# Issuing the six loads of each graph from GpSimd's queue instead of SyncE's, in a four-layer graph network

## The chip, the cores and the metric

The kernel runs on one core of a Trainium2 chip. The metric is the device time of one execution in microseconds (us); each kernel was run several times, and a run counts as fast when it lies within 1.5% of the fastest of its kernel. Profiles are of one execution each; its span can differ from the median time by some tenths of a per cent. PE is TensorE (matmuls), PEld its weight load, DVE is VectorE, ACT ScalarE, POOL GpSimd, SP SyncE; the letter q behind a name means that engine's queue of issued DMAs. A DMA lands when its completion is signalled.

## The reference

There are 64 independent graphs with 256 nodes and 512 features. Each goes through four layers, and each layer is added to its input:

```python
def reference(x, adj, nodemask, ...):          # x (64,256,512), adj (64,256,256), float32
    h = maximum(layernorm(x), 0);  x = x + gnn0(h, adj)   # softmax over nodes of sum(q k^T * adj), times v
    h = maximum(layernorm(x), 0);  x = x + gnn1(h, adj)   # 8-head attention, masked by adj
    h = maximum(layernorm(x), 0);  x = x + gnn2(h, adj)   # 8 heads, tanh(adj * xc xp^T), no softmax
    h = maximum(layernorm(x), 0);  x = x + gnn3(h, adj, nodemask)
    return x                                   # ... the weights are left out
```

## The kernel before

Each step of a graph is a small function that emits instructions. A plan gives every step a time, sorts the steps of all graphs by it, and pins each engine to the resulting order, so an engine never overtakes itself. Graphs follow one another by 60.2 of the plan's units, and a graph lives for nearly five periods, so five graphs are in flight.

Steps, with the line numbers by which the profile names them:

```python
@step("load")                                          # xt, adj and blocks are buffers of a pool
def _():
    nc.sync.dma_start(g.take("xt"), x[b]...)           # L633  512 KB
    nc.sync.dma_start(g.take("adj", 4), adj[b]...)     # L634  256 KB
    blocks = g.take("blocks")                          # adj again, in 32x32 blocks
    for q in range(4):
        nc.sync.dma_start(blocks[q*S:(q+1)*S], ...)    # L638  4 x 64 KB, rows of 256 B
@step("at")
    nc.vector.transpose(g.take("at", NC)..., g["blocks"]...)           # L643 VectorE
@step("st0")
    nc.vector.bn_stats(stats[:, c, :], g["xt"][:, c, :])               # L662 VectorE
@step("mxv")                                           # four small operations on mx, 128x16
    nc.vector.tensor_tensor(mx, mx, st["ec"]..., OP.add)               # L861
    nc.vector.tensor_scalar(low, mx, ...)                              # L863
    nc.vector.scalar_tensor_tensor(low, mx, 0.2, low, ...)             # L864
    nc.vector.tensor_tensor(mx, mx, low, OP.max)                       # L865
@step("eg2")
    nc.gpsimd.tensor_tensor(e, e, g["negt"]..., OP.add)                # L897 GpSimd, 2.35 us
@step("tv3")
    nc.vector.tensor_tensor(th[:, s], ..., g["at"], OP.mult)           # L1041 VectorE
@step("yg")
    nc.gpsimd.tensor_tensor(xt, xt, y, OP.add)                         # L1076, one half on GpSimd, one on VectorE
@step("am")                                            # waits for L1041, the last reader of at
    nc.gpsimd.tensor_scalar(g["at"]..., mask_c..., op0=OP.mult)        # L1087 GpSimd
```

In the plan "load" of one graph is at 180.6 of the graph three before it, right behind that graph's "am" at 180.09.

Of the kernel before, what the change touches and what calls it, by code (L numbers as in the profile page):

```python
# [20 lines left out]
NC = N // P  # L21
# [7 lines left out]
S = 32  # L29
# [354 lines left out]
class Graph:  # L384
# [5 lines left out]
    def step(self, name):  # L390
        def add(run):
            self.steps[name] = run
            return run
        return add
# [19 lines left out]
def tile_four_gnn_layers(ctx: ExitStack, tc: tile.TileContext, x, adj, nodemask,  # L414
# [6 lines left out]
    nc = tc.nc  # L421
# [203 lines left out]
    def graph(b):  # L625

        g = Graph(plan)
# [2 lines left out]

        @step("load")
        def _():
            nc.sync.dma_start(g.take("xt"), x[b].rearrange("(p c) d -> p c d", c=NC))  # L633
            nc.sync.dma_start(g.take("adj", 4), adj[b].rearrange("(p c) m -> p c m", c=NC))  # L634

            blocks = g.take("blocks")
            for q in range(4):
                nc.sync.dma_start(blocks[q * S:(q + 1) * S],  # L638
                                  adj[b].rearrange("(a i) (q e) -> q i a e", i=S, q=4)[q])

        @step("at")
# [520 lines left out]
```

## Time and profile before

| | kernel before |
|---|---|
| time, median of the 4 runs beside the kernel after | 3898.6 us (3894.8 to 3902.7) |
| span of the profiled run | 3884.0 us |
| TensorE busy | 98% |
| VectorE busy | 78% |
| GpSimd busy | 33% |
| steady period of a graph | 58.65 us |

The period is the mean of 41 intervals between starts of L643 in the steady part. The prediction below shows the busy shares, the chain of waits and the timelines of one steady graph. Two more lines are needed for later. The first is the table by stretches: window, its length, then busy time with the number of instructions for PE, PEld, DVE, ACT and POOL, then the granted TensorE clock, the DMA share and GB/s.

```profile
1000.00:3400.00 2400.00, 2399.22 (x10973) 1545.78 (x10972) 1912.00 (x4955) 1066.52 (x2050) 805.89 (x697) 1.00 0.63 189
```

TensorE is busy in 2399.22 of 2400 us. VectorE is busy 1912.00 of 2400, which is 46.7 us of a period of 58.65; it waits the other 11.9. The second thing is where VectorE's four small operations stand against GpSimd's work, in the timelines of VectorE and GpSimd (start, duration, us; in brackets the idle time before and what ended it):

```profile
1864.10 0.17 DVE L861 TENSOR_TENSOR mx<-mx,ec 128x16 f32<-128x16 f32 x1
1864.31 0.17 DVE L863 TENSOR_SCALAR mx<-mx 128x16 f32<-128x16 f32 x1
...
1866.72 1.72 POOL L1076 TENSOR_TENSOR xt<-xt,hn 128x512 f32<-128x512 f32 x1 [13.33 <-DMA hn<-sq_d]
```

They take 0.17 us each and are done 1.8 us before GpSimd's next instruction begins.

### The profile page before, as it was taken

Reading aid. Unit: us, or ns where it says so; the run is one execution under the profiler, and the core shown is the slowest. Engines: PE = TensorE matmul, PEld = TensorE weight load, DVE = VectorE, ACT = ScalarE, POOL = GpSimd, SP = SyncE. Lnnn points to the kernel's source line nnn. Section 1 sums busy time; section 2 is a strip of 40 time slices with the busy share of each in tenths; the row PEclk is TensorE's granted clock in tenths of the full one; section 3 lists DMA queues with packets and bytes.
Section 4 is the critical chain, followed back from the end, with each engine's and each line's share of the span. In section 5 each row is a group of like instructions: output and inputs, shape, how many; then the busy total and the mean of one; then the engine's idle time right before and its main releaser. Section 6 shows DMA issues by size and latency. Waiting matters only on the chain.

```text
span 3884.0 us, 53839 instructions
## 1 busy us (share of the span) xinstructions
PE 3809.3 (98%) x17218; PEld 2443.6 (63%) x17218; DVE 3025.1 (78%) x7769; ACT 1668.5 (43%) x3205; POOL 1264.8 (33%) x1100
## 2 busy tenths in 40 slices
PE   7999999999999999999999999999999999999989
PEld 4756666666666666666666666666666666665564
DVE  6887888878877877877888778778777778776774
ACT  2443444444444444444444444444444444443342
POOL 1332333333333323323323323323323333333231
PEclk9999999999999999999999999999999999999989
DMA  7565666665665665666666666666666666665543
GB/s 211 177 190 170 188 189 185 192 194 176 199 196 174 200 195 177 197 194 180 193 190 188 191 190 188 188 189 189 187 188 191 186 190 191 185 190 163 173 149 107
DMA packets 921353, 717.64 MB, mean 185 GB/s; under 512 B 783792, under 2 KB 821232, under 8 KB 896496
## 3 DMA queue, kind: packets, MB, share of 16 engines
q1 hardware_dynamic: 921072, 714.21, 60.8%
q8 instruction: 138, 2.26, 0.2%
q14 instruction: 143, 1.17, 0.1%
HBM read 477.56 MB, written 236.45 MB: 184 GB/s over the span
## 4 chain that ended last, share of the span: by engine, by line
PE 88%; DVE 6%; DMA 3%; issue 1%; SPq 1%; ACT 0%; POOL 0%; DVEq 0%; POOLq 0%; ACTq 0%
PE bank L611 55%; PE bank L921 12%; PE bank L1009 6%; PE bank L1023 5%; PE bank L1095 5%; PE bank L987 3%; DVE junk L851 2%; PE bank L773 1%; DMA sq_d<-sq 1%; DVE sq L617 1%; PE bank L723 1%; DMA all<-m_d 1%; DMA all<-er_d 1%; DVE pair L903 1%; DMA ht<-sq_d 1%
## 5 line engine op out<-in xcount | busy, mean ns | idle before, releaser
L611 PE MATMUL bank<-w_s,ht 128*128 128x256 f32 (+2 forms) x3072 | 949.9, 462 | 14.8 <-DMA ht<-sq_d 9.5
L611 PE MATMUL bank<-wv_s,ht 128*128 128x512 f32 x2048 | 916.6, 595 | 0.0
L611 PEld LDWEIGHTS bank<-w_s,ht 128*128 128x128 f32 x3072 | 595.3, 197 | 352.3 <-issue 237.9
L611 PEld LDWEIGHTS bank<-wv_s,ht 128*128 128x128 f32 x2048 | 393.0, 197 | 415.4 <-issue 400.9
L897 POOL TENSOR_TENSOR pair<-pair,negt 128x1024 f32<-128x1024 f32 x256 | 601.8, 2371 | 51.5 <-ACT pair L890 47.3
L685 ACT ACTIVATE hn<-xt,shift,rstd 128x512 f32<-128x512 f32 x512 | 388.8, 806 | 433.1 <-DVE shift L678 424.4
L921 PEld LDWEIGHTS bank<-feats,pair 128*128 128x128 f32 x4096 | 512.2, 200 | 54.3 <-issue 29.6
L1048 ACT ACTIVATE pair<-pair 128x512 f32<-128x512 f32 x512 | 299.2, 625 | 558.4 <-DVE pair L1041 558.1
L921 PE MATMUL bank<-feats,pair 128*128 128x65 f32 x4096 | 507.5, 283 | 17.5 <-ACT pair L909 17.5
L890 ACT ACTIVATE pair<-all,ec 128x256 f32<-128x256 f32 x1024 | 417.1, 494 | 229.6 <-DMA all<-er_d 225.6
L851 DVE CUSTOM_DVE_ANT_0 junk<-all,adj 128x256 f32<-128x256 f32 x1024 | 446.3, 436 | 38.2 <-DMA all<-er_d 4.8
L611 PE MATMUL bank<-m_s,ht 128*128 128x512 f32 x1024 | 466.3, 599 | 1.9 <-DMA ht<-sq_d 1.2
L673 POOL TENSOR_TENSOR rstd<-rstd,power 128x2 f32<-128x2 f32 x256 | 180.2, 704 | 845.7 <-DVE rstd L669 715.7
L1041 DVE TENSOR_TENSOR pair<-bank,at 128x512 f32<-128x512 f32 x512 | 325.8, 679 | 109.6 <-PE bank L1009 108.7
L617 DVE STREAM_TRANSPOSE sq<-hn 128x512 f32<-128x512 f32 x512 | 338.5, 694 | 59.9 <-ACT hn L685 59.7
L1076 POOL TENSOR_TENSOR xt<-xt,hn 128x512 f32<-128x512 f32 x64 | 108.2, 1691 | 840.8 <-DMA hn<-sq_d 712.1
L903 DVE TENSOR_TENSOR pair<-pair,all 128x1024 f32<-128x1024 f32 x256 | 309.8, 1230 | 57.6 <-DMA all<-m_d 53.7
L662 DVE BATCH_NORM_STATS2 stats<-xt 128x6 f32<-128x512 f32 x512 | 327.2, 681 | 34.2 <-POOL xt L1076 27.5
L611 PEld LDWEIGHTS bank<-m_s,ht 128*128 128x128 f32 x1024 | 195.9, 196 | 208.4 <-issue 202.3
L946 POOL TENSOR_TENSOR xt<-xt,o 128x256 f32<-128x256 f32 x256 | 183.8, 728 | 409.1 <-DVE o L938 300.8
L909 ACT ACTIVATE pair<-pair 128x1024 f32<-128x1024 f32 x256 | 262.3, 1047 | 55.3 <-DVE pair L903 49.9
L1009 PE MATMUL bank<-xc,xpt 64*128 64x256 f32 x2048 | 256.7, 390 | 0.9 <-ACT xc L995 0.7
(74 smaller groups left out, 3793.2 us busy)
## 6 DMA issues: line engine op xcount, KB each, us to landing
sq_d<-sq SPq DMA_DIRECT2D x384, 512.0 KB
ht<-sq_d SPq DMA_DIRECT2D x1024, 128.0 KB
all<-er_d SPq DMA_DIRECT2D x128, 1024.0 KB
all<-m_d SPq DMA_DIRECT2D x64, 1024.0 KB
xt<-in_x_dram SPq DMA_DIRECT2D x64, 512.0 KB
xpt<-sq_d SPq DMA_DIRECT2D x256, 128.0 KB
hn<-sq_d SPq DMA_DIRECT2D x256, 128.0 KB
out_dram<-xt SPq DMA_DIRECT2D x64, 512.0 KB
```

The lines of the kernel that those rows point to most:

```text
L611: nc.tensor.matmul(p, chunk(ht[:, k], c), w[:, k], start=(k == 0), stop=(k == KC - 1))
L617: nc.vector.transpose(sq.rearrange("p (r k i c) -> p c k r i", r=4, k=KC, c=NC)[:, c], t[:, c])
L662: nc.vector.bn_stats(stats[:, c, :], g["xt"][:, c, :])
L685: nc.scalar.activation(hn[:, c, :], g["xt"][:, c, :], AF.Relu, bias=st["shift"][:, c:c + 1], scale=st["rstd"][:, c:c + 1])
L851: nc.vector.tensor_tensor_reduce(junk, g["en"][:, h, :], g["adj"][:, c, :], 1.0, -BIG, OP.add, OP.max, g["mx"][:, c, h:h + 1])
L890: nc.scalar.activation(e[:, s, j, :], g["es"][:, h, :], AF.Prelu, bias=st["ec"][:, j, H + h:H + h + 1], alpha=0.2)
L897: nc.gpsimd.tensor_tensor(e, e, g["negt"][:, None].to_broadcast([P, 2, NC, N]), OP.add)
L903: nc.vector.tensor_tensor(e, e, g["m"][:, 2 * p:2 * p + 2, None, :].to_broadcast([P, 2, NC, N]), OP.subtract)
L921: nc.tensor.matmul(po[:, h % 4, :], chunk(e[:, s, j], i), feats[:, j, h, :], start=(j == 0), stop=(j == NC - 1))
L1009: nc.tensor.matmul(ps[s][:, m, :], chunk(g["xpt"][half, p], m), g["xc"][half, p, :], start=True, stop=True)
L1041: nc.vector.tensor_tensor(th[:, s], g[f"ps{p}{s}"].rearrange("p (m n) -> p m n", m=NC), g["at"], OP.mult)
L1048: nc.scalar.activation(g[f"th{p}"][:, s], g[f"th{p}"][:, s], AF.Tanh)
```

## The change

The intent is to relieve SyncE's queue, which issues all DMAs of the kernel, by giving the loads to an engine that is busy a third of the time.

```diff
         @step("load")
         def _():
-            nc.sync.dma_start(g.take("xt"), x[b].rearrange("(p c) d -> p c d", c=NC))
-            nc.sync.dma_start(g.take("adj", 4), adj[b].rearrange("(p c) m -> p c m", c=NC))
+            nc.gpsimd.dma_start(g.take("xt"), x[b].rearrange("(p c) d -> p c d", c=NC))
+            nc.gpsimd.dma_start(g.take("adj", 4), adj[b].rearrange("(p c) m -> p c m", c=NC))
 
             blocks = g.take("blocks")
             for q in range(4):
-                nc.sync.dma_start(blocks[q * S:(q + 1) * S],
+                nc.gpsimd.dma_start(blocks[q * S:(q + 1) * S],
                                   adj[b].rearrange("(a i) (q e) -> q i a e", i=S, q=4)[q])
```

## The prediction

> **What bounds the kernel now.** I read the page of the profile first, then the timeline of each engine over two neighbouring graphs in the middle, then the waits by tile. The page says that TensorE is the bound and that nothing else is near:
>
> ```profile
> PE 3809.3 (98%) x17218; PEld 2443.6 (63%) x17218; DVE 3025.1 (78%) x7769; ACT 1668.5 (43%) x3205; POOL 1264.8 (33%) x1100
> ...
> PE 88%; DVE 6%; DMA 3%; issue 1%; SPq 1%; ACT 0%; POOL 0%; DVEq 0%; POOLq 0%; ACTq 0%
> ```
>
> The first line is busy time, the second the chain that ended last. TensorE has 2% to gain, so no relief of a queue can be worth more than about 75 us of 3884, and DMA is 3% of the chain. What can move the time is a wait that reaches TensorE in every graph. There are 64 graphs, five in flight, and each engine's instructions run in the fixed order of a plan. In the steady part everything repeats every 58.60 us (the transpose of the adjacency starts at 1849.65 and again at 1908.25).
>
> In the timeline of SyncE's queue, the six loads of one graph are issued here (start, duration, both us):
>
> ```profile
> 1837.32 0.56 SPq L633 DMA_DIRECT2D xt<-in_x_dram  x1
> 1838.22 0.92 SPq L634 DMA_DIRECT2D adj<-in_adj_dram  x1
> 1839.20 1.90 SPq L638 DMA_DIRECT2D blocks<-in_adj_dram  x4
> ```
>
> The first to use them is VectorE, which transposes `blocks` at L643 and takes the statistics of x at L662. From its timeline:
>
> ```profile
> 1847.27 1.25 DVE L1041 TENSOR_TENSOR pair<-bank,at 128x512 f32<-128x512 f32 x2
> 1848.44 1.29 DVE L617 STREAM_TRANSPOSE sq<-hn 128x512 f32<-128x512 f32 x2
> 1849.65 0.67 DVE L643 STREAM_TRANSPOSE at<-blocks 128x512 f32<-128x512 f32 x1
> 1850.24 0.72 DVE L1116 SCALAR_TENSOR_TENSOR bank<-bank,mask_c,cols 128x512 f32<-128x512 f32 x1
> ```
>
> L643 has no idle time before it. The load was issued 1849.65 - 1837.32 = 12.3 us earlier, and by 1841.10 all six were out. Over the whole run L643 waited 0.5 us for its blocks, once. That lead is what the kernel lives on. GpSimd's timeline in the same place:
>
> ```profile
> 1840.20 0.70 POOL L673 TENSOR_TENSOR rstd<-rstd,power 128x2 f32<-128x2 f32 x1 [3.39 <-DVE rstd L669]
> 1848.62 1.83 POOL L1087 TENSOR_SCALAR at<-at,mask_c 128x256 f32<-128x256 f32 x2 [7.72 <-DVE pair L1041]
> 1850.43 0.62 POOL L649 TENSOR_SCALAR adj<-adj 128x512 f32<-128x512 f32 x1
> ```
>
> It sits idle for 7.72 us at L1087, because its queue is in order and that instruction needs VectorE's L1041, which ended at 1848.52.
>
> **What the Trainium skill says.** "DMA: Bandwidth & Descriptors", section "Issuing engines are not separate DMA queues": DMAs of all issuing engines run on the same 16 DMA engines and interleave, so another issuer saves only issue time. Here that is 0.56 + 0.92 + 1.90 = 3.4 us of SyncE's queue per graph, and SyncE's queue then waits from 1841.10 to 1847.38 for VectorE anyway. The same page, "Anatomy of one DMA", fits a DMA of GpSimd's path as about 2.0 us plus bytes / 436e3; the trace of before has no GpSimd DMA to compare. "Perfetto Trace Analysis", section "DMA Instruction — SWDGE (GPSIMD)": two of GpSimd's cores generate the descriptors, so such a DMA passes through the engine's own instruction stream, behind its semaphore waits. The trace shows that stream to be in order, by the 7.72 us above.
>
> **The change, part by part.** It removes nothing from the work: the same 1.05 MB per graph (512 + 256 + 4 x 64 KB). It removes 384 issues from SyncE and adds 384 to GpSimd. Comparing the order of the instructions of the two built kernels: TensorE, VectorE and ScalarE are the same line by line. On GpSimd, in 52 of 64 graphs the load now stands directly behind L1087 and ahead of L649. The other twelve, in the filling and draining, stand elsewhere, two of them at the very start.
>
> Step 1, when the load is issued. L1087 ends at 1850.43. In before, SyncE issued at 1837.32, so the load comes 13.1 us later, and 0.8 us *after* the moment at which VectorE wants to start L643. All the lead is gone.
>
> Step 2, from issue to landing. L643 waits for all four `blocks` DMAs, the last of the six. With the skill's fit, if generation costs nothing and all overlap, 2.0 + 1.05e6 / 436e3 = 4.4 us; if the six fixed parts come one after another, 6 x 2.0 + 2.4 = 14.4 us. Each `blocks` DMA has 32 x 8 rows of 256 B, twice the rows of x or adj, which speaks for the upper half; at this time also SyncE has two 1 MB broadcasts in flight (issued 1850.29 to 1851.41). I choose 11.5 us, an estimate from the page's fit.
>
> Step 3, VectorE. It stands from 1849.65 to about 1850.43 + 11.5 = 1861.9, that is 12.3 us in every steady graph. It has 58.6 x 0.2 = 12 us idle per graph, but the stall is at a place where it had none, and what follows is on a chain.
>
> Step 4, what reaches TensorE. Its timeline and SyncE's after the transpose:
>
> ```profile
> 1857.17 7.03 PE L611 MATMUL bank<-wv_s,ht 128*128 128x512 f32 x16
> 1864.04 7.03 PE L611 MATMUL bank<-w_s,ht 128*128 128x512 f32 x16
> 1870.90 0.38 PE L723 MATMUL bank<-ident,wc 128*128 128x128 f32 x2
> 1871.12 2.05 PE L611 MATMUL bank<-wqk_s,ht 128*128 128x128 f32 x16
> ```
>
> ```profile
> 1858.01 2.59 SPq L705 DMA_DIRECT2D sq_d<-sq  x1
> 1860.78 2.17 SPq L1069 DMA_DIRECT2D hn<-sq_d  x4
> 1864.20 2.54 SPq L622 DMA_DIRECT2D ht<-sq_d  x4
> ```
>
> TensorE has work that needs nothing of VectorE from 1849.65 to 1864.04, 14.4 us. Then three things come from behind the transpose: the PSUM banks and `ht` for the matmuls at 1864.04 (SyncE's write of `sq` at 1854.09 stands ahead of that gather and itself waits for VectorE), L1116's score for 1870.90, and the new graph's own `ht` for 1871.12. The last chain is the longest: statistics from 1850.88, normalised rows, transpose ended 1856.74 (7.1 us after L643 began), write issued at 1858.01, gather issued 1864.20 to 1866.74, and about 3.3 us to land (the broadcast of 1 MB issued at 1874.13 was waited for until 1879.08, 4.9 us; half the bytes land sooner), which is 1870.0. So this chain has 1871.12 - 1870.0 = 1.1 us of slack. With the stall, SyncE's queue is empty when the late `sq` arrives, which gives back perhaps 1.7 of the 1.3 + 2.6 us that this write spent behind other issues and in its own. TensorE then loses 12.3 - 1.1 - 1.7 = 9.5 us per graph.
>
> Step 5, does it repeat? Yes: the next L1087 waits for VectorE's L1041, which needs matmuls of TensorE that come after the late `wqk_s` matmuls in its order. So nothing can run ahead to rebuild the lead; the load is inside the loop now.
>
> Sum: 52 x 9.5 = 494 us. For the ten other graphs that are neither first nor second, a quarter of it each, 10 x 2.4 = 24 us. 3899 + 518 = 4417, rounded to 4420 us.
>
> **Rivals.** (a) The load is hidden anyway, the time is the same: 12.3 us of lead and GpSimd at 33% speak for it. Against it, the lead is measured on SyncE's queue, and GpSimd's order puts the issue behind the consumer's planned start; with any latency at all the wait is there. It would give 3900. (b) SyncE's queue is relieved and things land earlier: DMA is 3% of the chain and TensorE's waits for `ht` are 10.6 us in all, so at best 3860. (c) Quick generation: landing 6 us after issue makes a stall of 6.8, and 4 us lost per graph, about 4120. (d) GpSimd's generation per row is slow, and L of step 2 is 17 us: a loss of 15 us per graph, about 4720. GpSimd would still not be the bound by sum (19.7 us busy per graph now), only by latency. "SBUF — State Buffer", box on the "DVE blocks DMA" trap, says VectorE's two-port operations lock GpSimd out of writing descriptors; since VectorE stands still while these are written, I expect little of it.
>
> **Range and chances.** Between (c) and (d) lies nearly everything: step 2 sets it, each us there being worth some 55 us. A range of 4180 to 4720 holds L from about 7 to 17 us. Faster needs the reading of the order to be false: 0.02. Same needs a landing within some 3 us of issue, or slack that I don't see: 0.04. Slower: 0.94.
>
> **What would show it.** In the changed profile, SyncE has no L633 to L638; GpSimd's issues of them come right behind L1087; L643 on VectorE shows idle time ended by the DMA of `blocks`, about 12 us per graph, some 600 us in all; TensorE's busy share falls towards 88%, its idle time standing before L611 with `wqk_s` (released by `ht`) or before L723; and the steady period is about 68 us. VectorE, ScalarE and GpSimd keep their busy times. I am wrong in step 1 if L643 doesn't wait; in step 2 if its wait is under 7 or over 17 us; in step 4 if TensorE loses much less than VectorE waits, or loses it at another place; and in step 5 if the period goes back to 58.6 us after some graphs.

## More of the kernel before

Twelve of the 64 (the pipeline's filling and draining) have tables of their own; the other 52 use this one:

```python
PERIOD = 60.2
TIMES = {
    "load": 0.000, "at": 1.247, "st0": 5.280, ...      # load, transpose of adj, statistics of x
    "mxv": 78.317, "ea2": 80.651, "eg2": 82.397, ...   # end of the maximum; first pair addition
    "tv3": 180.071, "ta3": 180.091, "am": 180.092, ... # 180.6 is where the graph three later loads
}
```

## The result, and the profile after

| | before | after |
|---|---|---|
| time, median | 3898.6 us | 4510.6 us (4502.6 to 4516.6, 4 runs) |
| ratio, 95% interval | | 1.1568 (1.1546 to 1.1591) |
| span of the profiled run | 3884.0 us | 4514.8 us |
| steady period | 58.65 us | 70.87 us |
| mean wait at L643 in it | 0 | 12.46 us |

Ratios here are the mean time of one kernel's fast runs over that of the other's of the same rounds, so they are not quite the ratio of the medians. The change makes the kernel 15.7% slower. From the page of the kernel after: busy times, the chain that ended last, and two groups of instructions (count, busy us, mean ns of one, then idle time before them and what ended it).

```profile
PE 3976.6 (88%) x17218; PEld 2489.8 (55%) x17218; DVE 3173.1 (70%) x7769; ACT 1661.8 (37%) x3205; POOL 1473.7 (33%) x1484
...
DVE 33%; PE 30%; DMA 13%; issue 13%; POOL 8%; ACT 1%; SPq 1%; DVEq 0%; POOLq 0%; ACTq 0%
...
L611 PE MATMUL bank<-w_s,ht 128*128 128x256 f32 (+2 forms) x3072 | 1065.5, 503 | 412.1 <-DMA ht<-sq_d 287.8
...
L643 DVE STREAM_TRANSPOSE at<-blocks 128x512 f32<-128x512 f32 x64 | 45.4, 709 | 632.1 <-DMA blocks<-in_adj_dram 632.1
```

The chain was 88% TensorE; now it goes round over VectorE, TensorE, the DMA and GpSimd. ("issue" in it is time in which an engine waited for nothing that the profile shows; GpSimd's DMA issues count as POOL.) L643 waits 632.1 us for its blocks, about the whole loss (the spans differ by 630.8). Note also the third engine of the first line: VectorE (DVE) is busy 148 us longer than in the kernel before (3173.1 against 3025.1), although its instructions are the same. The GpSimd timeline of one steady graph, which answers to the one in the prediction:

```profile
2069.30 1.84 POOL L1087 TENSOR_SCALAR at<-at,mask_c 128x256 f32<-128x256 f32 x2 [7.72 <-DVE pair L1041]
2071.09 0.65 POOL L633 DMA_DIRECT2D xt<-in_x_dram  x1
2071.74 0.55 POOL L634 DMA_DIRECT2D adj<-in_adj_dram  x1
2072.28 2.36 POOL L638 DMA_DIRECT2D blocks<-in_adj_dram  x4
...
2097.74 2.34 POOL L897 TENSOR_TENSOR pair<-pair,negt 128x1024 f32<-128x1024 f32 x1
```

The six issues take 3.55 us of GpSimd's time and come only when L1087 is through. The VectorE timeline beside it:

```profile
2069.12 1.29 DVE L617 STREAM_TRANSPOSE sq<-hn 128x512 f32<-128x512 f32 x2
2082.20 0.71 DVE L643 STREAM_TRANSPOSE at<-blocks 128x512 f32<-128x512 f32 x1 [11.79 <-DMA blocks<-in_adj_dram]
...
2096.68 1.13 DVE L861 TENSOR_TENSOR mx<-mx,ec 128x16 f32<-128x16 f32 x1
2097.84 2.27 DVE L863 TENSOR_SCALAR mx<-mx 128x16 f32<-128x16 f32 x1
...
2138.09 1.25 DVE L1041 TENSOR_TENSOR pair<-bank,at 128x512 f32<-128x512 f32 x2
```

VectorE is ready for L643 at 2070.41 (2069.12 + 1.29) and gets it at 2082.20. Then look at L861 and L863: two operations of 0.17 us now take 1.13 and 2.27 us. L863 ends at 2100.11, and GpSimd's L897 beside it at 2100.08; L861 ends at 2097.81 where GpSimd's L1076 (2096.51, 1.26 us) ends. VectorE is held until GpSimd's instruction ends. (The last line, L1041, is what the next graph's L1087 waits for.) The TensorE timeline:

```profile
2077.84 7.03 PE L611 MATMUL bank<-wv_s,ht 128*128 128x512 f32 x16
2092.53 8.96 PE L611 MATMUL bank<-w_s,ht 128*128 128x512 f32 x16 [7.66 <-DVE mx L851]
2101.33 0.27 PE L723 MATMUL bank<-ident,wc 128*128 128x128 f32 x1
```

TensorE's long idle time is before the matmuls with `w_s`. The bracket names L851, whose result they don't read; of the 412.1 us of such waits in the page's line above, 287.8 are put down to the DMA of `ht`. This `ht` is gathered by SyncE at 2087.09, behind a write of `sq` at 2086.68 that itself waits for VectorE's L1057. And these matmuls take 8.96 us instead of 7.03: in the table by stretches the granted clock (the third number from the right) is 0.58 in the 4.5 us behind the idle time.

```profile
2092.50:2097.00 4.50, 4.47 (x6) 2.00 (x7) 4.19 (x19) 2.46 (x7) 0.49 (x1) 0.58 0.79 218
```

"TensorE: Matmul & The Clock Gate" of the Trainium skill, section "Part 1: The HAM clock gate (the "warmup" mystery)", says that TensorE falls to half clock after an idle window of about 3.4 us and comes back after as long a busy one; this trace agrees: after 7.66 us of idle time the clock is 0.58 in the window shown, and 1.00 from 2097.00 to 2101.50.

Now the balance. For the same 2400 us in the middle of the kernel after:

```profile
1000.00:3400.00 2400.00, 2089.24 (x9057) 1303.96 (x9056) 1675.09 (x4096) 877.39 (x1696) 775.33 (x777) 0.93 0.50 156
```

Busy time of VectorE per graph is 1675.09 / 2400 x 70.87 = 49.5 us. A period of VectorE, whose stream is in order, is its busy time, plus its wait for the load, plus its other waits (all in us per graph):

| kernel | period | busy | wait for the load | other waits |
|---|---|---|---|---|
| before | 58.65 | 46.72 | 0 | 11.93 |
| after | 70.87 | 49.46 | 12.46 | 8.95 |
| difference | +12.22 | +2.74 | +12.46 | -2.98 |

So the other waits did give back 3.0 us, and VectorE's own instructions took 2.7 us of that away. By lines: the give-back is at VectorE's L1076 (its wait for `hn` falls from 1.87 to 0.01 us), L662, L728 and L903 (0.35 to 0.42 us each); the growth is in L861 to L865, together 0.71 us before and 3.37 after. Such a balance is arithmetic and could be drawn up for any engine; that VectorE's is the one that counts is for the experiments to show.

The loop can be added up as well (means of the same 41 periods). From the start of L643 to the end of the last L1041 ahead of the next load VectorE takes 57.19 us, against 57.51 in the kernel before. Then come 0.10 us until L1087 starts, 1.84 us of L1087, and 11.73 us from there to the next L643: together 70.86.

### The profile page after: what moved, and what is told of

The parts are those of the page before. It is cut to its first block, busy times and chain, and to the rows that moved or that the text cites.

```text
span 4514.8 us, 53905 instructions
## 1 busy us (share of the span) xinstructions
PE 3976.6 (88%) x17218; PEld 2489.8 (55%) x17218; DVE 3173.1 (70%) x7769; ACT 1661.8 (37%) x3205; POOL 1473.7 (33%) x1484
## 4 chain that ended last, share of the span: by engine, by line
DVE 33%; PE 30%; DMA 13%; issue 13%; POOL 8%; ACT 1%; SPq 1%; DVEq 0%; POOLq 0%; ACTq 0%
PE bank L611 11%; DMA blocks<-in_adj_dram 10%; PE bank L921 10%; DVE junk L851 8%; DVE stats L662 4%; DVE sq L617 4%; PE bank L1009 3%; DVE shift L678 2%; PE bank L1095 2%; PE bank L987 2%; POOL at L1087 2%; POOL blocks L638 2%; DVE mx L863 2%; DVE pair L1041 2%; POOL rstd L673 2%
## 5 line engine op out<-in xcount | busy, mean ns | idle before, releaser
L611 PE MATMUL bank<-w_s,ht 128*128 128x256 f32 (+2 forms) x3072 | 1065.5, 503 | 412.1 <-DMA ht<-sq_d 287.8
L611 PEld LDWEIGHTS bank<-w_s,ht 128*128 128x128 f32 x3072 | 633.0, 211 | 834.4 <-DVE mx L851 449.3
L611 PE MATMUL bank<-wv_s,ht 128*128 128x512 f32 x2048 | 918.1, 596 | 11.1 <-DVE feats L819 4.6
L897 POOL TENSOR_TENSOR pair<-pair,negt 128x1024 f32<-128x1024 f32 x256 | 602.2, 2372 | 35.2 <-ACT pair L890 30.9
L673 POOL TENSOR_TENSOR rstd<-rstd,power 128x2 f32<-128x2 f32 x256 | 180.3, 704 | 1017.9 <-DVE rstd L669 1017.0
L643 DVE STREAM_TRANSPOSE at<-blocks 128x512 f32<-128x512 f32 x64 | 45.4, 709 | 632.1 <-DMA blocks<-in_adj_dram 632.1
L851 DVE CUSTOM_DVE_ANT_0 junk<-all,adj 128x256 f32<-128x256 f32 x1024 | 451.4, 441 | 34.7 <-DMA all<-er_d 1.6
L1041 DVE TENSOR_TENSOR pair<-bank,at 128x512 f32<-128x512 f32 x512 | 326.0, 680 | 106.7 <-PE bank L1009 105.5
L662 DVE BATCH_NORM_STATS2 stats<-xt 128x6 f32<-128x512 f32 x512 | 327.0, 680 | 18.8 <-DMA xt<-in_x_dram 11.7
L903 DVE TENSOR_TENSOR pair<-pair,all 128x1024 f32<-128x1024 f32 x256 | 312.2, 1239 | 38.5 <-DMA all<-m_d 33.0
L1076 POOL TENSOR_TENSOR xt<-xt,hn 128x512 f32<-128x512 f32 x64 | 89.7, 1402 | 690.1 <-DMA hn<-sq_d 676.3
```

Of the source, the lines that this page charges most:

```text
L611: nc.tensor.matmul(p, chunk(ht[:, k], c), w[:, k], start=(k == 0), stop=(k == KC - 1))
L673: nc.gpsimd.tensor_tensor(st["rstd"], st["rstd"], power, OP.pow)
L851: nc.vector.tensor_tensor_reduce(junk, g["en"][:, h, :], g["adj"][:, c, :], 1.0, -BIG, OP.add, OP.max, g["mx"][:, c, h:h + 1])
L897: nc.gpsimd.tensor_tensor(e, e, g["negt"][:, None].to_broadcast([P, 2, NC, N]), OP.add)
L903: nc.vector.tensor_tensor(e, e, g["m"][:, 2 * p:2 * p + 2, None, :].to_broadcast([P, 2, NC, N]), OP.subtract)
L1041: nc.vector.tensor_tensor(th[:, s], g[f"ps{p}{s}"].rearrange("p (m n) -> p m n", m=NC), g["at"], OP.mult)
```

## The experiments

All kernels gave the right result. The calls did not all run on the same chip, so kernels of different calls are compared by their ratios to "before", the kernel before in the same rounds: 3893.7 us in the first call, 3899.6 in the second, 3898.9 in the third, 3898.2 in the fourth.

**Place or issuer?** The first call separates the place in the order from the engine that issues.

*gp_early*: the kernel after, with the load just ahead of L1087 in GpSimd's order.

```diff
-    "load": 0.000, "at": 1.247, ...
+    "load": -0.800, "at": 1.247, ...
```

> The six loads stay on GpSimd, but one place earlier in the plan of the 52 steady graphs: ahead of L1087 instead of behind it, so GpSimd can issue them in the 7.7 us in which it stood waiting there. Theory of the place (the loss is the wait of L643 on VectorE, because the issue stands behind L1087): the issue comes some 8 us earlier, L643 waits under 2 us per graph, TensorE hardly loses, time 3900 to 3990. Rival (GpSimd's path itself costs the time[...]): over 4200, near 4510.

Measured: 3909.1 us, ratio 1.0038 (1.0023 to 1.0053). The GpSimd timeline:

```profile
2029.49 0.65 POOL L633 DMA_DIRECT2D xt<-in_x_dram  x1
...
2037.12 1.84 POOL L1087 TENSOR_SCALAR at<-at,mask_c 128x256 f32<-128x256 f32 x2 [4.06 <-DVE pair L1041]
```

VectorE's beside it, without idle time before L643:

```profile
2038.14 0.68 DVE L643 STREAM_TRANSPOSE at<-blocks 128x512 f32<-128x512 f32 x1
```

The issue is now in the 7.7 us that GpSimd waits anyway, 8.65 us before L643 starts (2038.14), and no steady graph waits for it: the period is 58.71 us, against 58.65. What follows: in the steady part GpSimd as an issuer costs next to nothing, and the place is what costs. Relieving SyncE gave nothing either, since the period did not fall. The blocks landed 3.8 us after their issue (median), while in the kernel after they need 8.6. The 0.4% that remains is outside the steady part: the intervals of the first graphs are longer by up to 3 us each, and VectorE waited for x three times, 11.1 us in all.

*sp_late*: the opposite. SyncE issues as in the kernel before, but at the late place.

```diff
-    "load": 0.000, "at": 1.247, ...     # kernel before
+    "load": 1.000, "at": 1.247, ...
```

> The loads go back to SyncE, but late: in its queue behind the four small DMAs of L834, which before issued at 1847.38 to 1849.09, some 12 us later than before and 1.3 us before GpSimd's issue in the changed kernel. Theory of the place: L643 waits about 6 us per graph[...], VectorE stands, and what is over the slack of about 4 us reaches TensorE: 4000 to 4200. Rival (GpSimd's path itself is at fault): the time of before, 3900.

Measured: 4184.0 us, ratio 1.0742 (1.0724 to 1.0760). Its waits view (engine and line, what it waited for, total us, times, longest):

```profile
DVE at L643 <- DMA blocks<-in_adj_dram: 301.3, 53, 8.1
```

L643 waits 5.78 us per steady graph and the period is 64.44 us, 5.79 more. So with no GpSimd DMA at all, a late issue loses as much as VectorE waits.

*gp_blocks* and *gp_x_adj*: only the four `blocks` loads, or only x and adj, go to GpSimd.

```diff
 gp_blocks: L638 by nc.gpsimd, L633 and L634 by nc.sync
 gp_x_adj:  L633 and L634 by nc.gpsimd, L638 by nc.sync
```

> Only the four DMAs of blocks are issued by GpSimd, x and adj by SyncE in their old place. Theory: L643 still waits, but for four issues and a quarter of the bytes: about 7 us instead of 12 per graph, of which about 4 are slack, time 4050 to 4200. If the wait for blocks alone were the whole of it, whatever else is issued: near 4510. If blocks had nothing to do with it: 3900.

> Only x and adj are issued by GpSimd (two DMAs, 768 KB), blocks by SyncE in its old place. Theory: L643 no longer waits, but L662, 1.2 us further on in VectorE's order, waits for x instead, about 6 to 8 us per graph: 4050 to 4250. If blocks were the only load that matters: 3900.

Measured: gp_blocks 4405.6 us, ratio 1.1316 (1.1298 to 1.1334); gp_x_adj 4269.3 us, ratio 1.0960 (1.0940 to 1.0980). Both are slower than I expected. The waits view of gp_x_adj:

```profile
DVE stats L662 <- DMA xt<-in_x_dram: 399.0, 52, 9.8
```

Here L643 does not wait but the next reader does, 7.7 us in each of 52 graphs, and the period is up by 7.35 us. In gp_blocks L643 waits 10.64 us and the period is up by 10.43, with a median landing of 7.0 us for a quarter of the bytes. So the time to land is not set by the bytes of the load, and either group alone makes a loss; but in each of the four kernels the loss of a period is the wait itself, to within 0.4 us. This is no law: sp_late, gp_blocks and gp_x_adj have 49.6 to 49.9 us of busy time and 8.5 to 9.1 us of other waits per graph, so, as in the kernel after, VectorE's longer instructions take back what its other waits give.

**Where did the slack go?** The prediction expected some of the wait to be given back. The second call tests two suspects in the kernel after: the cold TensorE, and the collision of L863 with GpSimd's L897.

*after_warm*: eight matmuls whose result is overwritten run in front of the `w_s` matmuls, in 53 graphs, to keep the clock up.

```diff
+    if not c and 4 <= b <= 56:
+        for _ in range(8):
+            nc.tensor.matmul(bank, ident, w2_s[:, 0], start=True, stop=True)
     rows(bank, g["ht"], c, w2_s)
```

*after_eg2*: the first pair addition on GpSimd comes behind the next L673, to be out of the way of L863. *after_warm_eg2*: both. *sp_late_eg2*: the same move in sp_late.

```diff
-    "ea2": 80.651, "eg2": 82.397,
+    "ea2": 80.651, "eg2": 86.200,
```

> The changed kernel with eight matmuls too many (identity times weights, overwritten by the real ones) at the place where TensorE stood idle 7.7 us and then ran at a granted clock of 0.50 to 0.58, in 53 graphs. The result stays right. Theory of the clock: the matmuls behind the wait run at full clock and take 7.0 instead of 9 to 10 us; if nothing else waits at that place, some 2 us less per graph, about 4405; if L1116 on VectorE, held up by GpSimd, takes over as the next wait, only some 0.5 to 1 us, about 4470. Rival (the lower clock has nothing to do with the idle time, or costs nothing): 4510 or slower by the added work.

> The changed kernel with one GpSimd addition (L897 of the third head pair) moved behind the next L673, so that it cannot run at the same time as VectorE's four small instructions L861 to L865, of which one takes 2.27 us instead of 0.17 in the changed kernel. Theory of the collision: those fall back to 0.17 us each, VectorE's next 2 to 3 us come earlier; TensorE, which is late for another reason, gains 0.4 to 1 us per graph, 4460 to 4490. Rival (the length of these is something else): no change in L863 and L864, 4510.

> Both of the above. Theory: clock and collision are the two terms that the prediction left out, and together they are worth about the 2.2 us by which the loss per graph (11.7 us) was over the forecast (9.5 us): 4380 to 4420. Rival: no more than the better of the two alone.

> The late load on SyncE (4184 us) with the same addition of GpSimd moved. There TensorE stood 2.5 us per graph before L723, waiting for L1116, which came behind the slowed instructions L861 to L865. Theory of the collision: most of this goes, 52 x 2 to 2.5 us: 4050 to 4090. Rival: 4184.

| kernel | time, us | ratio to before (95%) | period | busy | wait for the load | other waits |
|---|---|---|---|---|---|---|
| after_warm | 4551.0 | 1.1678 (1.1655 to 1.1700) | 71.12 | 49.55 | 12.53 | 9.04 |
| after_eg2 | 4489.9 | 1.1525 (1.1492 to 1.1557) | 70.31 | 48.96 | 12.33 | 9.02 |
| after_warm_eg2 | 4541.4 | 1.1656 (1.1625 to 1.1686) | 71.04 | 49.38 | 12.62 | 9.04 |
| sp_late_eg2 | 4175.9 | 1.0718 (1.0694 to 1.0742) | 64.16 | 49.30 | 5.69 | 9.17 |

The last two were to gain 100 us or so and missed, and so did after_warm, which was to gain 40 or more. after_warm did keep the clock: the `w_s` matmuls took 7.11 us again. The period did not fall, so a cold TensorE is not what sets it. (Of its 40 us extra over the kernel after, some 13 are in the steady part.) after_eg2 met its forecast at the edge (4460 to 4490). It removed most of the collision it aimed at (L863 fell from 1.43 to 0.26 us; L861, beside L1076, still took 0.77), and made another one: VectorE's L903 took 6.4 us per graph instead of 4.9, because the moved GpSimd addition now falls on it. All four leave VectorE's busy time within 0.5 us of 49.46.

**Which stream sets the period?** The third call has two more tests on the kernel after, and a candidate on the kernel before.

*after_bcast*: the two 1 MB broadcasts that SyncE has in flight beside the load are issued later. The gather for `w_s` is placed just ahead of them.

```diff
-    "enes": 67.749,      "ht2": 134.926,
+    "enes": 74.200,      "ht2": 134.100,
```

> The kernel after with the two 1 MB broadcasts that share the DMA engines with the load (the one before VectorE's max operations and the one behind the gather for xp0) issued by SyncE about 6.5 us later, so that the load's transfers have the engines to themselves for longer. Theory that the long landing is contention with the broadcasts: the blocks land some 4 to 6 us after their issue instead of 8.6, VectorE waits 7.5 to 9.5 us at the transpose instead of 12.4. If the loss stays equal to the wait, 4300 to 4400 us; the broadcasts come later, which may cost it back at the max operations (4400 to 4600). Rival, that a load from GpSimd's queue lands slowly whatever else is under way: landing still 8 us or more, wait about 12.4, 4500 or slower.

Measured: 4573.4 us, ratio 1.1733 (1.1707 to 1.1758). The contention is real. In the view of tile `blocks`:

```profile
DMA to landing us min/median/max: 2.5/4.5/6.5
```

The landing fell from a median of 8.6 to 4.5 us by moving nothing but other transfers, and the wait at L643 from 12.46 to 7.88 us. The rival, that GpSimd's loads are slow by themselves, is out as the reason for the 8.6 us. But the time did not follow, since the broadcast is now late for L851, the first of VectorE's maximum operations, which waits 6.8 us per graph for it; the period is 71.74 us. The wait was moved along VectorE's stream, not removed: VectorE's stretch of the loop is 62.65 us instead of 57.19.

*after_at_on*: L643 and the statistics come later in VectorE's order, behind L1057 and the bias additions, so that SyncE's write and gather for the `w_s` matmuls don't stand behind VectorE's wait.

```diff
-    "at": 1.247,  "st0": 5.280,  "rs0": 5.300,  "negt": 7.670,
+    "at": 11.400, "st0": 11.450, "rs0": 11.460, "negt": 11.470,
```

> The kernel after, with the transpose of blocks moved about 2 us of work later in VectorE's order: the two bias additions and the transpose of cols, which TensorE's and SyncE's next work waits for, come before it. Theory that a graph's period is VectorE's rigid stream of about 58.4 us plus the wait: the wait falls by the work moved ahead, to 9.5 to 10.5 us, and the period by the same; 52 graphs by 2 to 3 us, 4360 to 4420 us. Rival, that the loss is TensorE's, because the gather for xp0 is held up behind the wait: with that gather freed TensorE works through the wait, and the loss falls by far more than the wait does, to 4100 to 4250 us. Second rival, that nothing depends on the order there: 4510 us.

Measured: 4566.3 us, ratio 1.1714 (1.1695 to 1.1734). The TensorE timeline, in a graph whose L643 started at 1902.80:

```profile
1904.22 7.11 PE L611 MATMUL bank<-w_s,ht 128*128 128x512 f32 x16 [2.49 <-DVE stats L662]
1911.17 0.27 PE L723 MATMUL bank<-ident,wc 128*128 128x128 f32 x1
1921.01 0.47 PE L723 MATMUL bank<-ident,wc 128*128 128x128 f32 x1 [9.56 <-DVE bank L1116]
```

TensorE starts `w_s` 1.4 us after L643 instead of 10.3, at full speed. All of it is lost two instructions later, where TensorE waits 9.56 us for VectorE's second L1116, which stands behind the maximum operations in VectorE's order. I had expected 4360 to 4420 from the wait alone, or 4100 to 4250 if TensorE's hold-up at `w_s` were the loss; both missed. The wait fell to 9.67 us as expected, but the other waits rose to 12.08: the work moved ahead had filled gaps behind L643 that now stand empty (L678 waits 1.98 us instead of 1.12), and L1057 waits 1.96 us where it waited for nothing. Busy time was 50.09: L851 takes 2.4 us more, its last two 1.36 and 2.44 us instead of 0.42 while GpSimd's L1076 and L897 run.

The test is not as clean as it looks, for it also delayed the load. From GpSimd's first issue to L643 the kernel after takes 11.8 us (mean), this one 13.6, and a block lands in 10.5 us (median) instead of 8.6. SyncE's write and gathers, freed, now run beside it:

```profile
1891.88 7.35 SPq L622 DMA_DIRECT2D ht<-sq_d  x4
```

VectorE's stretch of the loop became 0.9 us shorter (56.33), the load 1.8 us longer, and the period 1.0 longer. What the test does show is that time given to TensorE at `w_s` comes to nothing, since TensorE then waits for VectorE.

*start_split*: the kernel before, with ScalarE's queue issuing the loads of graphs 0 and 1 only, as an attempt to beat both.

```diff
+    eng = nc.scalar if b < 2 else nc.sync
-    nc.sync.dma_start(...)        # all six
+    eng.dma_start(...)
```

> The kernel before, with the loads of graphs 0 and 1 alone issued by ScalarE's queue, which is idle at the start, so that the weights that SyncE brings come about 6 us earlier; from graph 2 on nothing changes. Theory that the start is held up by SyncE issuing one transfer after another: 3 to 8 us faster, 3887 to 3893 us, ratio about 0.998 to 0.9995. Rival, that the start is bound by the DMA engines themselves, 60 to 90% busy there: within 2 us of the kernel before, ratio 1.000.

Measured: 3897.9 us, ratio 1.0000 (0.9987 to 1.0014): nothing gained. The profile shows one reason, and it is the main case in small: ScalarE's first activation waited behind its own twelve issues and began at 12.61 us, against 7.22 us before.

**The contention by itself.** *after_held*: one tiny GpSimd instruction that reads what L865 wrote is put in front of GpSimd's L1076, so that neither it nor L897 can start before VectorE's four small operations are through.

```diff
+    @step("hold")                       # at 81.000 in TIMES
+    def _():
+        held = work.tile([P, 2], F32, name="held", bufs=1)
+        nc.gpsimd.tensor_scalar(held, g["mx"][:, 0, :2], 1.0, None, op0=OP.mult)
```

> The kernel after with one tiny GpSimd instruction added in each of the graphs in the steady part: it reads what VectorE's last operation on mx wrote, so that GpSimd's L1076 and the first pair addition behind it can't start before VectorE's four small operations on mx (L861 to L865) are done. These four took 0.53 us in a graph of the kernel before and 3.2 us in the kernel after, because GpSimd's work now falls on them. Theory that a graph's period is VectorE's own stream (busy time plus its waits), and that this contention took back what the other waits gave: the four take 0.7 us or less together, the wait for the blocks stays at 12.4 us, the other waits rise by at most 0.8 us because GpSimd's work is later, and the period falls from 70.9 us by 1.5 to 2.5 us; 52 graphs make 80 to 130 us, so 4380 to 4435 us. Rival, that TensorE's lower clock after its idle time is what the period follows: 4490 us or more.

Measured: 4428.7 us (4408.2 to 4440.6), ratio 1.1357 (1.1311 to 1.1402), which is 82 us less than the kernel after (by the ratios, too: 1.1568 - 1.1357 = 0.0211 of 3898), by *adding* a wait. Timelines of VectorE and GpSimd (L1081 and L902 are L1076 and L897 of the others):

```profile
2060.68 0.17 DVE L863 TENSOR_SCALAR mx<-mx 128x16 f32<-128x16 f32 x1
...
2061.37 0.69 POOL L870 TENSOR_SCALAR held<-mx 128x2 f32<-128x2 f32 x1 [11.60 <-DVE mx L865]
2062.03 1.26 POOL L1081 TENSOR_TENSOR xt<-xt,hn 128x512 f32<-128x512 f32 x1
2063.26 2.35 POOL L902 TENSOR_TENSOR pair<-pair,negt 128x1024 f32<-128x1024 f32 x1
```

Its table by stretches:

```profile
1000.00:3400.00 2400.00, 2117.18 (x9285) 1334.20 (x9285) 1632.99 (x4214) 898.12 (x1738) 816.02 (x831) 0.94 0.52 161
```

The period is 69.11 us = 47.02 busy + 12.42 for the load + 9.67 other waits. The four operations take 0.72 us, as in the kernel before; the busy time is down by 2.44 us, the other waits are up by 0.72, and the period is down by 1.76; VectorE's stretch of the loop is 55.48 us instead of 57.19. 50 graphs x 1.76 = 88 us, of which the measured times show 82. The rival, the lower TensorE clock, asked for 4490 us or more.

None of the twelve beats the kernel before.

## Why the prediction was right or wrong

The direction, the main cause (the late issue and VectorE's stall) and the range held. The sum was 94 us short (4417 against 4510.6), and it was short in one term.

- **Step 1, the issue: right.** L633 is issued at 2071.09 behind L1087, 0.68 us after VectorE was ready for L643; predicted 0.8. gp_early shows that this place is the cause: moved ahead of the same instruction, the load costs the steady part nothing.
- **Step 2, issue to landing: right in size.** 2082.20 - 2071.09 = 11.1 us from the first issue to L643, predicted 11.5. The fit gave 4.4 to 14.4 us, and the reason for which I went to the upper half, many short rows, is not shown; so near a hit is luck. What is shown is contention with SyncE's two broadcasts: 8.6 us for a block beside them, 4.5 with them later, 3.8 in gp_early.
- **Step 3, VectorE's stall: right.** 12.46 us per steady graph and 632.1 in all, predicted 12.3 and some 600.
- **Step 4, "TensorE then loses 12.3 - 1.1 - 1.7 = 9.5 us per graph": the term that failed.** The loss is 12.2. Relief was there: VectorE's other waits shrank by 3.0 us, close to my 2.8, but at other places, so that the agreement is luck: 1.86 of it is at L1076, whose gather SyncE issues 8.4 us after L643 instead of 11.1. But GpSimd's half of L1076 and its L897 then come earlier too, onto VectorE's small operations, and VectorE's instructions grew by 2.7 us. The mis-sized term is the give-back net of contention: 2.8 predicted, 3.0 - 2.7 = 0.2 measured. The prediction named the interference of VectorE and GpSimd, in one direction only, against descriptor writing, and said that the engines "keep their busy times"; VectorE's rose by 148 us. after_held shows that the contention is worth 82 us of the time, 1.76 us of the 2.7 per graph that the sum was short. In after_held the wait is 12.42 us and the period's loss 69.11 - 58.65 = 10.46, so the net give-back is 2.0, still under my 2.8; what makes up that last part no run takes apart.
- **Step 4, the place: wrong.** TensorE's long idle time is before the matmuls with `w_s`, not with `wqk_s`. I had called the new graph's own chain the longest, but the `sq` write behind L1057 reaches TensorE first. after_at_on shows that this place does not set the period: freed there, TensorE waits for L1116 instead. With after_warm, which gained nothing, and after_held, where 2.44 us less of VectorE's busy time took 1.76 off the period, the runs speak for VectorE's stream, in order and with the wait in it, as what sets the period.
- **Step 5, repetition: right.** The next L1087 waits for an L1041 that comes behind the same stall, and the lead is not rebuilt. In the profile 50 graphs wait some 12 us, not 52; their 50 intervals are together 609.5 us longer than before, 12.2 each. The other 21 of the 630.8 us between the spans are in the filling and draining, where I had put 24.

The rival of a hidden load (a) fails by the place, (b) by gp_early's unchanged period. (c) and (d) were about the landing, and it lay between them. Nor is the trap that the prediction named to be seen: the six issues take GpSimd 3.55 us in the kernel after, where VectorE stands still, and 3.56 in gp_early, where it works for 1.66 us of them. Not settled is why the blocks alone land only 1.6 us sooner than among all six (7.0 against 8.6 us), and x without the blocks no sooner at all (8.7 us in both): no run takes apart how the loads share the DMA engines with the broadcasts and gathers.

## What to carry to other kernels

In a kernel whose engines run in a fixed order, moving a DMA to another issuer moves it behind everything that this engine waits for: look at the new queue's neighbours first, and place the issue in a wait that the engine has anyway. When a wait enters an in-order stream, idle time elsewhere in it (VectorE had 11.9 us of 58.65) need not take it up: count all of the wait as lost until a balance of that stream (busy time, this wait, other waits) says otherwise. And when work on a shared path shifts, see what it falls on: a wait that is given back can start another engine's instruction just where it blocks you.

## What the Trainium skill lacked or had wrong

- "DMA: Bandwidth & Descriptors", "Issuing engines are not separate DMA queues", says that several issuers save only issue time. It lacks the other side: the same load cost 0.4% ahead of one GpSimd instruction (3909.1 us) and 15.7% behind it (4510.6 us).
- The same page's fit for a DMA of GpSimd's path has no term for traffic in flight (elsewhere the page says that the fixed part shrinks with a lighter load): blocks of 64 KB landed in 3.8 us in gp_early, and in 8.6 us beside two broadcasts of 1 MB. "Anatomy of one DMA" calls the generation of descriptors small and has no figure for how long it holds GpSimd; each issue took 0.55 to 0.65 us of GpSimd's time here, six took 3.55.
- "SBUF — State Buffer", "Who interferes with whom", says that a VectorE instruction with two SBUF inputs, or in a two-port mode, and a GpSimd instruction that reads SBUF block each other fully, and that whoever issues first holds the ports for its whole instruction. This trace agrees (L861, of two inputs, 1.13 us beside L1076; L863 2.27 us, begun 0.10 us after an L897 of 2.34; 0.17 each alone); whether L863 ran in a two-port mode is not shown. What it lacks is an example of what this costs very small operations: 0.71 us of work became 3.37 us per graph, and keeping GpSimd back from them gained 82 us of the run.
